# Macaron block on one core: first-pair score maxima started three block steps later, router logits of four tiles in one step

## The chip, the core and the metric

One core of a Trainium2 chip runs the whole program. The metric is device time in microseconds, and lower is better. Five engines work side by side, each through its own queue in order: PE (TensorE, matmul, with its weight loads shown as PEld), DVE (VectorE), ACT (ScalarE), POOL (GpSimd) and SP (SyncE, which here only issues DMAs). Semaphores connect them.

## The reference

The input is 8 sequences of 1024 tokens of 256 numbers, all fp32. Three layers follow each other, each on a layer norm of x:

```python
x = x + 0.5 * ffn(layernorm(x))
x = x + attention(layernorm(x))
x = x + 0.5 * ffn(layernorm(x))

# attention: 16 heads of 16
xd = (x @ W_down).reshape(b, t, h, s)
keys    = einsum('bthk,hik->bthi', xd, tokeys) * scale     # queries, values alike
attn    = softmax(einsum('bqhs,bkhs->bhqk', queries, keys))
out     = einsum('bhqk,bkhs->bqhs', attn, values).reshape(b, t, e) @ W_unify + b_unify

# ffn: one expert of 8 a token, at most 320 tokens an expert, the rest through one shared network
probs = softmax(xf @ router_w + router_b); eid = argmax(probs)
rank  = cumsum(onehot)[.., eid] - 1;       valid = rank < 320
out   = where(valid, expert[eid](xf), relu(xf @ ow1 + ob1) @ ow2 + ob2)
```

The softmax is computed with its maximum taken off, and a token's place in its expert depends on all tokens before it.

## The kernel before

Three stages follow each other: the first feed-forward layer, attention, and the second feed-forward layer. In each, the order of the instructions on PE, ACT and DVE is the order in which Python emits them (a manual schedule), so a generator's `yield` decides which work lies next to which.

**The feed-forward layers** run in blocks of 512 tokens (`Layer.blocks`, L433). A block is sixteen steps between yields: eight steps that multiply into the hidden layer (`ph_o`, L456) and eight that multiply out of it (`pe_o`, L499), where the four tiles of 128 tokens take two steps each, of 10 and of 6 matmul records. The finished rows are scattered to DRAM by a POOL DMA (L512).

**Attention** goes over 32 pairs, 8 sequences times 4 groups of 4 heads. A pair is sixteen steps `u` (called steps of attention here), and each step does two things for different pairs (`passes`, L956): the exponentials of pair n (three matmuls `psc` a head, the last of which brings in the row minima `m`, then an exponential on ACT), and the maxima of pair n + 1 (two matmuls `pm` a head, then a reduction `halves` on DVE, L1003). In between, the previous step's exponentials are multiplied with the values (`av`, L1018). After eight steps `lowest` (L931) makes the minima of half a pair, and `spread` (L944) sends them through DRAM into the rows `m` with two DMAs on SP (L948, L949). `fetch(n)` (L919) loads keys and queries of pair n with three DMAs on SP: two for keys (L926) and one for queries (L929).

**Work beside attention.** Everything else that attention needs is kept as generators in the list `beside`: `prepare` (the projections of the next sequence), `unify` (the output projection), `stats`, `biased`, and `route` (the second layer's router). Each is labelled with what its next piece needs most: ARRAY, DVE or POOL, and has a pair by which it is due. A step of attention may take one ARRAY piece (in 8 or 6 of the 16 steps of a pair, `SLOTS_OF`, L776), one DVE piece (in 6 or 8 of them), and a POOL piece if it took no ARRAY piece. What is not done when its pair ends is emitted there at once (`done_by`, L1148). A step that takes an ARRAY piece, or is one of the first two of its half pair, multiplies with the values in one go; others do it in two halves around the second group of scores.

`route(b)` (L1080) normalizes, transposes four tiles (`ptrn`, L832), multiplies them with the router's weights (`found`, L1087: 16 matmul records of 8 columns in `pl`, L1091), and again for the next four tiles. Then `places` (L270) finds the slots with two small groups of matmuls, `inside` and `behind` (L304, L326); after each, DVE waits for three additions on POOL. At last eight tiles are normalized and sent by POOL.

**The first pair.** The maxima of pair 0 have no exponentials to run beside. They are taken in 32 pieces of 4 matmuls while the last four blocks of the first feed-forward layer run, one after each block step (`first_pair`, L1183). The block steps are numbered 0 to 64; in each, one ARRAY, two DVE and one POOL piece may be taken. `prepare(0)` ends and `fetch(0)` is issued a few block steps ahead of the first piece; the yields behind `fetch(0)` set how many:

```python
                yield from prepare(0)
                fetch(0)
                yield POOL
                yield POOL
                for u in range(UNITS):
                    for order in ORDERS:
                        yield ARRAY
                        passes(None, 0, u, order, {})
```

When the blocks are done, every engine goes through a branch (L668) that skips a rarely needed rest, and `run` (L1230) starts with `fetch(1)`.

Of the kernel before, what the change touches and what calls it, by code (L numbers as in the profile page):

```python
# [40 lines left out]
def macaron(  # L41
# [80 lines left out]
    def clearing(pool, on=nc.gpsimd):  # L122

        zero = pool.tile([P, W], F32, tag="zero", name="zero")
        on.memset(zero, 0.0)
        nc.gpsimd.iota(
            zero[:, D : D + 1].bitcast(I32), pattern=[[1, 1]], base=N, channel_multiplier=1
        )
        return zero
# [10 lines left out]
    ARRAY, DVE, POOL = 0, 1, 2  # L140

    def norm_steps(name, b, mean, rstd):


        st = small.tile([P, TB, 6], F32, tag="st", name=f"st_{name}")
        mv = small.tile([P, TB, 2], F32, tag="mv", name=f"mv_{name}")
        for t in range(TB):
            nc.vector.bn_stats(st[:, t, :], xs[b][:, t, :])
            nc.vector.bn_aggr(mv[:, t, :], st[:, t, :])
            yield DVE  # L150
        nc.vector.tensor_copy(mean, mv[:, :, 0])
        v = small.tile([P, TB], F32, tag="v", name=f"v_{name}")
        nc.vector.tensor_scalar(v, mv[:, :, 1], EPS, None, ALU.add)

        half = small.tile([P, TB], I32, tag="half", name=f"half_{name}")
        nc.vector.tensor_single_scalar(
            half, v.bitcast(I32), 1, ALU.logical_shift_right
        )
        yi = small.tile([P, TB], I32, tag="yi", name=f"yi_{name}")
        nc.vector.tensor_scalar(  # L160
            yi, half, -1.0, float(0x5F3759DF), ALU.mult, ALU.add
        )
        y = yi.bitcast(F32)
        for i in range(4):
            if i % 2 == 0:
                yield DVE
            a = small.tile([P, TB], F32, tag="a", name=f"a_{name}_{i}")
            nc.vector.tensor_tensor(a, y, y, ALU.mult)
            nc.vector.scalar_tensor_tensor(a, a, -0.5, v, ALU.mult, ALU.mult)
            to = rstd if i == 3 else small.tile(  # L170
                [P, TB], F32, tag="yn", name=f"yn_{name}_{i}"
            )
            nc.vector.scalar_tensor_tensor(to, a, 1.5, y, ALU.add, ALU.mult)
            y = to
        yield POOL
# [5 lines left out]
    def normed(pool, tag, name, t, mean, rstd, on=None, numbered=False):  # L181
        xn = pool.tile([P, W if numbered else D], F32, tag=tag, name=name)
        on = on or nc.vector
        on.tensor_scalar(xn[:, :D], xt(t), mean, rstd, ALU.subtract, ALU.mult)
        if numbered:
            nc.gpsimd.tensor_copy(
                xn[:, D:].bitcast(I32), number[:, t : t + 1].to_broadcast([P, W - D])
            )
        return xn
# [571 lines left out]
    def attention(use, weights, router):  # L761
# [29 lines left out]
        def bank_v(name):  # L791

            return use.pm.tile([P, 512], F32, tag="pm", name=name)
# [17 lines left out]
        def rows_transposed(name, b, mean, rstd, used):  # L811

            def rows(q):
                return [
                    normed(
                        use.pool, "xn", f"{name}_{b}_{t}", b * TB + t, mean[:, t : t + 1],
                        rstd[:, t : t + 1], nc.gpsimd,
                    )  # L820
                    for t in range(4 * q, 4 * q + 4)
                ]

            ready = rows(0)
            yield POOL
            yield ARRAY
            for q in range(2):
                to = use.pool.tile([P, KC, 512], F32, tag="xnt", name=f"T{name}_{b}_{q}")
                for k in range(KC):
                    ps = bank(f"pt{name}_{b}_{q}_{k}")  # L830
                    for i, r in enumerate(ready):
                        nc.tensor.transpose(  # L832
                            ps[:, i * P : (i + 1) * P], r[:, k * P : (k + 1) * P], ident
                        )
                    nc.scalar.copy(to[:, k, :], ps)
                if q == 0:
                    ready = rows(1)
                yield
                yield from used(q, to)
# [240 lines left out]
        def route(b):  # L1080

            sl = slice(b * TB, (b + 1) * TB)
            mean, rstd = router.mean[:, sl], router.rstd[:, sl]
            yield from norm_steps(f"f1_{b}", b, mean, rstd)
            logits = use.pool.tile([P, TB, E], F32, tag="logits", name=f"logits1_{b}")

            def found(q, xnt):  # L1087
                pl = bank_v(f"pl_{b}_{q}")
                for i in range(4):
                    for k in range(KC):  # L1090
                        nc.tensor.matmul(  # L1091
                            pl[:, i * E : (i + 1) * E],
                            lhsT=xnt[:, k, i * P : (i + 1) * P],
                            rhs=rw_sb[:, k, :],
                            start=(k == 0),
                            stop=(k == KC - 1),
                        )
                    if i == 1:
                        yield
                nc.vector.tensor_tensor(  # L1100
                    logits[:, 4 * q : 4 * q + 4, :],
                    pl[:, : 4 * E].rearrange("p (t e) -> p t e", e=E),
                    rb_sb.unsqueeze(1).to_broadcast([P, 4, E]),
                    ALU.add,
                )
                yield ARRAY if q == 0 else DVE

            yield from rows_transposed("rn", b, mean, rstd, found)
            yield from router.places(b, logits, use.pool, bank_v, nc.gpsimd)
            for t in range(b * TB, (b + 1) * TB):  # L1110

                xn = normed(
                    use.pool, "send", f"send1_{t}", t, *router.of(t),
                    nc.gpsimd if b < B - 2 else nc.vector, numbered=True,
                )
                router.send(t, xn)
                yield POOL

        def stats(b):

            sl = slice(b * TB, (b + 1) * TB)
            yield from norm_steps(f"a{b}", b, amean[:, sl], arstd[:, sl])
# [4 lines left out]
        def afterwards(n=0):  # L1127

            for _ in range(len(later) - n):
                later.pop(0)()  # L1130
# [42 lines left out]
        def ones(i):  # L1173
            vp = use.pool.tile([P, TB * HEADS * V + S], F32, tag=f"vp{i}", name=f"vp{i}")
            nc.gpsimd.memset(vp, 1.0)
            vps.append(vp)

        def zero_rows(i):
            m = use.pool.tile([P, 512], F32R, tag=f"m{i}", name=f"m{i}")
            nc.gpsimd.memset(m.bitcast(F32), 0.0)  # L1180
            ms.append(m)

        def first_pair(others):  # L1183

            for i in range(2):
                zero_rows(i)
            ones(0)  # L1190
            zero = clearing(use.pool)

            def steps():

                for _ in range(6):
                    yield POOL
                yield DVE
                yield from stats(0)
                yield POOL
                yield from prepare(0)  # L1200
                fetch(0)
                yield POOL
                yield POOL
                for u in range(UNITS):
                    for order in ORDERS:
                        yield ARRAY
                        passes(None, 0, u, order, {})
                    if u % TB == TB - 1:
                        lowest(0, u // TB)
                    elif u % TB == 0:  # L1210
                        afterwards()
                yield DVE
                afterwards()

            beside.append([0, POOL, steps()])
            for i, _ in enumerate(others):

                if i in (10, 29, 36):

                    reload((10, 29, 36).index(i) + 1)  # L1220
                if i in (17, 36, 43):
                    again = (17, 36, 43).index(i) + 1
                    beside.append([again + 1, DVE, stats(again)])
                if i in (44, 52):
                    clear(zero, 1, *((0, SLOTS) if i == 44 else (SLOTS + SURE, ROWS)))
                for kind in (ARRAY, DVE, DVE, POOL):
                    step(kind)
            done_by(B)
# [185 lines left out]
```

## Time and profile before

| what | value |
|---|---|
| time, median of 3 runs | 2935.99 us (2933.0 to 2938.25) |
| the profiled execution's own time | 2939.6 us |
| its span, first to last instruction | 2937.9 us |
| mean granted TensorE clock | 0.981 |
| PE busy | 2799.3 us (95%) |
| DVE busy | 1883.1 us (64%) |
| ACT busy | 1375.2 us (47%) |
| POOL busy | 851.8 us (29%) |
| attention proper, first psc to last av | 660.5 to about 2450 us |

The span is 1.7 us shorter than the profiled execution's time, and that execution is 3.6 us longer than the median. The clock column of a profile is the share of full TensorE speed that was granted in a stretch; the hardware records when it changes.

### The profile page before, as it was taken

How to read it: one execution, taken by the hardware profiler on the slowest of the kernel's cores; microseconds unless marked ns; L12 is line 12 of the kernel's file. 1: busy time of each engine (PE TensorE's matmuls, PEld its weight loads, DVE VectorE, ACT ScalarE, POOL GpSimd, SP SyncE). 2: the span in 40 equal slices, each digit the busy share in tenths (PEclk: the TensorE clock that was granted, in tenths of full speed). 3: DMA queues.
4: the chain of work that ended last, by engine and by line, in shares of the span. 5: the costliest groups of instructions: out<-in, count | busy, mean ns of one | idle time of the engine just before them, and what ended most of it. 6: DMA issues, size and time to landing. Idle time of an engine off the chain costs nothing.

```text
span 2937.9 us, 56693 instructions
## 1 busy us (share of the span) xinstructions
PE 2799.3 (95%) x22066; PEld 1546.2 (53%) x22066; DVE 1883.1 (64%) x4189; ACT 1375.2 (47%) x2512; POOL 851.8 (29%) x1136
## 2 busy tenths in 40 slices
PE   4799999899999999999999999999999999999998
PEld 4567776454444444444444444444444445666775
DVE  7344223467897888888788788788788963212221
ACT  1111111207766666766766765766766663111111
POOL 3434433414001033123222321420420214432331
PEclk7799999999999999999999999999999999999999
DMA  7522553413112101301301301311321102321440
GB/s 224 152 83 78 176 187 99 161 47 121 53 58 97 67 24 60 124 24 56 128 24 52 133 24 42 125 41 39 125 80 38 39 3 73 128 61 49 150 147 28
DMA packets 163737, 251.47 MB, mean 86 GB/s; under 512 B 36737, under 2 KB 109698, under 8 KB 163458
## 3 DMA queue, kind: packets, MB, share of 16 engines
q1 hardware_dynamic: 144178, 196.93, 20.6%
q0 software_dynamic: 18432, 50.62, 5.1%
q8 instruction: 177, 2.90, 0.4%
q14 instruction: 102, 0.84, 0.1%
q10 hardware_dynamic: 848, 0.18, 0.0%
HBM read 144.10 MB, written 103.57 MB: 84 GB/s over the span
## 4 chain that ended last, share of the span: by engine, by line
PE 63%; DVE 13%; issue 1%; DMA 0%; POOL 0%; ACT 0%; POOLq 0%; DVEq 0%
PE psc L987 20%; PE av L1018 15%; DVE halves L1003 9%; PE pm L987 6%; PE pe_o L499 5%; PE ph_o L456 5%; PE pe_e L499 2%; PE ph_e L456 2%; PE pu L1063 2%; PE pxd L862 2%; PE pv L894 1%; DVE turned L1033 1%; PE pq L880 1%; PE pl L1091 1%; PE ptrn L832 0%
## 5 line engine op out<-in xcount | busy, mean ns | idle before, releaser
L1003 DVE TENSOR_REDUCE halves<-pm 128x1 f32<-128x512 f32 x2048 | 1309.3, 681 | 260.9 <-PE pm L987 239.6
L996 ACT ACTIVATE ex<-psc 128x512 f32<-128x512 f32 x2048 | 1111.4, 596 | 574.5 <-PE psc L987 570.9
L987 PE MATMUL pm<-k,q 32*128 32x512 f32 x4096 | 870.5, 448 | 50.6 <-DVE halves L1003 38.6
L987 PE MATMUL psc<-q,k 32*128 32x512 f32 x4096 | 791.8, 455 | 3.1 <-PEq L668 3.1
L1018 PE MATMUL av<-ex,vp 128*32 128x256 f32 (+1 forms) x6472 | 610.9, 449 | 0.0
L987 PEld LDWEIGHTS psc<-q,k 32*128 32x128 f32 x4096 | 326.6, 183 | 479.0 <-issue 423.1
L987 PEld LDWEIGHTS pm<-k,q 32*128 32x128 f32 x4096 | 374.9, 183 | 133.4 <-DVE halves L1003 107.3
L987 PE MATMUL psc<-m,ones_r 32*128 32x512 f32 x2048 | 406.9, 390 | 0.0
L456 PE MATMUL ph_o<-bT_o,oa 128*128 128x512 f32 x704 | 318.6, 601 | 7.1 <-DVE h_o L474 5.3
L499 PE MATMUL pe_o<-ob,h_o 128*128 128x256 f32 x1408 | 322.6, 386 | 0.0
L1041 POOL TENSOR_TENSOR ot<-turned,rec 128x256 f32<-128x256 f32 x64 | 39.7, 620 | 883.9 <-DVE rec L1036 875.6
L499 PEld LDWEIGHTS pe_o<-ob,h_o 128*128 128x128 f32 x1408 | 268.1, 193 | 48.5 <-issue 13.8
L1018 PEld LDWEIGHTS av<-ex,vp 128*32 128x32 f32 x6472 | 127.6, 108 | 298.3 <-issue 275.6
L456 PEld LDWEIGHTS ph_o<-bT_o,oa 128*128 128x128 f32 x704 | 131.2, 191 | 159.7 <-issue 147.4
L470 ACT ACTIVATE h_o<-ph_o,ob 128x512 f32<-128x512 f32 x88 | 60.5, 687 | 328.9 <-PE ph_o L456 305.0
L987 PEld LDWEIGHTS psc<-m,ones_r 32*128 32x128 f32 x2048 | 196.6, 184 | 13.0
L474 DVE TENSOR_SCALAR h_o<-ph_o,ob 128x512 f32<-128x512 f32 x88 | 65.9, 748 | 196.2 <-ACT h_o L470 179.4
L509 DVE SCALAR_TENSOR_TENSOR y_o<-pe_o,old_o 128x256 f32<-128x256 f32 x88 | 37.2, 423 | 205.8 <-PE pe_o L499 141.2
L499 PE MATMUL pe_e<-wb,h_e 128*128 128x256 f32 (+1 forms) x640 | 143.9, 381 | 0.0
L456 PE MATMUL ph_e<-bT_e,wa 128*128 128x320 f32 x512 | 140.6, 433 | 1.8 <-ACT bT_e L204 1.8
L204 ACT COPY bT_o<-pt_bT_o 128x1024 f32<-128x1024 f32 x22 | 22.3, 1012 | 250.8 <-PE pt_bT_o L200 225.9
L499 PEld LDWEIGHTS pe_e<-wb,h_e 128*128 128x128 f32 (+1 forms) x640 | 112.9, 179 | 16.4 <-issue 3.1
(183 smaller groups left out, 2385.1 us busy)
## 6 DMA issues: line engine op xcount, KB each, us to landing
k<-krows SPq DMA_DIRECT2D x64, 512.0 KB
wa<-in_w_dram SPq DMA_DIRECT2D x16, 1024.0 KB
wb<-in_w_dram SPq DMA_DIRECT2D x16, 1024.0 KB
krows<-kh SPq DMA_DIRECT2D x32, 512.0 KB
krows<-kl SPq DMA_DIRECT2D x32, 512.0 KB
q<-qrows SPq DMA_DIRECT2D x32, 512.0 KB
rows_o<-buf SPq DMA_DIRECT2D x88, 130.0 KB
x<-in_x_dram SPq DMA_DIRECT2D x8, 1024.0 KB
```

Source lines behind the costliest of these rows:

```text
L456: nc.tensor.matmul(ps[:, i * 512 : i * 512 + width], lhsT=wa[:, k, (m + i) * P : (m + i + 1) * P], rhs=xnt[:, k, c0:c1], start=(k == 0), s ...
L470: nc.scalar.activation(t[:, 0, : hi - lo], ps[:, lo - c0 : hi - c0], AF.Relu, bias=bias[:, m : m + 1],)
L474: nc.vector.tensor_scalar(t[:, 1, : hi - lo], ps[:, 512 + lo - c0 : 512 + hi - c0], bias[:, m + 1 : m + 2], 0.0, ALU.add, ALU.max,)
L499: nc.tensor.matmul(ps[lo - i * P : hi - i * P, :D], lhsT=of[:, lo - a : hi - a], rhs=w[:, m, :], start=(m == 0), stop=(m == MC - 1),)
L509: nc.vector.scalar_tensor_tensor(y[:n, :], ps[:n, :D], 0.5, olds[i][:n, :], ALU.mult, ALU.add)
L862: nc.tensor.matmul(ps, lhsT=wd_sb[:, k, m * P : (m + 1) * P], rhs=xnt[:, k, :], start=(k == 0), stop=(k == KC - 1),)
L987: nc.tensor.matmul(ps, lhsT=lhs, rhs=rhs, start=(len(left) + 1 == todo[kind, h, "of"]), stop=not left,)
L996: nc.scalar.activation(ex, ps, AF.Exp, scale=S ** -0.5)
L1003: nc.vector.tensor_reduce(halves[m][:, t, half, h : h + 1], ps, AX.X, ALU.max, negate=True)
L1018: nc.tensor.matmul(avs[n, q][32 * h : 32 * h + 32, cols], lhsT=vps[b % 2][:, at : at + 2 * S], rhs=ex[:, cols], start=(c == 0), stop=(c == ...
L1041: nc.gpsimd.tensor_tensor(outs_t[q][:, :, at : at + S].rearrange("p (t a) s -> p a t s", t=4), by[:, :, :S].rearrange("p (a t) s -> p a t ...
L1063: nc.tensor.matmul(ps[:, i * D : (i + 1) * D], lhsT=outs[b, g, q][:, at : at + P], rhs=wu_sb[:, g, :], start=(g == 0), stop=(g == G // 2 - 1),
```

## The change

Two edits. In `first_pair`, five POOL yields instead of two follow `fetch(0)`, so that the first of the 32 pieces of maxima comes three block steps later, and so do all pieces after it. In `route`, `found` no longer yields in the middle of its four tiles, so that its 16 matmul records are one ARRAY piece, where they were two of 8 records; a router pass takes two ARRAY pieces fewer, and whatever stands behind it in `beside` moves up.

```diff
--- before.py
+++ after.py
@@ -1095,8 +1095,6 @@
                             start=(k == 0),
                             stop=(k == KC - 1),
                         )
-                    if i == 1:
-                        yield
                 nc.vector.tensor_tensor(
                     logits[:, 4 * q : 4 * q + 4, :],
                     pl[:, : 4 * E].rearrange("p (t e) -> p t e", e=E),
@@ -1199,8 +1197,9 @@
                 yield POOL
                 yield from prepare(0)
                 fetch(0)
-                yield POOL
-                yield POOL
+
+                for _ in range(5):
+                    yield POOL
                 for u in range(UNITS):
                     for order in ORDERS:
                         yield ARRAY
```

## The prediction

> **What bounds the kernel now.** I read the page's chain first, then PE's and SP's timelines around the end of the first layer, then the clock by windows.
>
> ```profile
> PE 63%; DVE 13%; issue 1%; DMA 0%; POOL 0%; ACT 0%; POOLq 0%; DVEq 0%
> ```
>
> The set end is PE's, with DVE second, so I price both edits on PE and ask where DVE ends a wait. PE at the first pair (timeline: start, length, instruction, idle before it and its releaser):
>
> ```profile
> 541.02 5.78 PE L499 MATMUL pe_o<-ob,h_o 128*128 128x256 f32 x26
> 554.43 1.22 PE L987 MATMUL pm<-k,q 32*128 32x512 f32 x4 [7.63 <-DMA q<-qrows]
> 555.58 2.93 PE L499 MATMUL pe_o<-ob,h_o 128*128 128x256 f32 x6
> ...
> 645.93 0.92 PE L987 MATMUL pm<-k,q 32*128 32x512 f32 x4
> 646.78 10.63 PE L499 MATMUL pe_o<-ob,h_o 128*128 128x256 f32 x48
> 660.51 0.79 PE L987 MATMUL psc<-q,k 32*128 32x512 f32 x2 [3.10 <-PEq L668]
> ```
>
> PE stands 7.63 us for the queries, and the blocks behind the first piece stand with it. The last piece comes 48 block records ahead of the end; then come the branch's 3.1 us. SP meanwhile:
>
> ```profile
> 648.76 0.33 SPq L948 DMA_DIRECT2D mrows<-lowturned  x1
> 650.17 0.64 SPq L949 DMA_DIRECT2D m<-mrows  x1
> 652.89 0.81 SPq L926 DMA_DIRECT2D k<-krows  x2
> 653.75 0.42 SPq L929 DMA_DIRECT2D q<-qrows  x1
> ```
>
> Keys and queries of pair 1 are asked for only behind the last minima. Their packets in the trace end at 659.1 us, one straggler at 660.5; PE wants them at 660.6. Two waits end within 0.2 us of each other, and one is not seen.
>
> Windows of the granted clock (length, busy time and count of PE, PEld, DVE, ACT, POOL, then PEclk):
>
> ```profile
> 553.71:557.12 3.41, 2.69 (x8) 1.80 (x9) 1.29 (x2) 0.00 (x0) 0.00 (x0) 0.50 0.00 1
> 557.13:560.53 3.40, 3.40 (x10) 1.90 (x9) 1.26 (x3) 0.00 (x0) 1.00 (x1) 0.50 0.00 0
> 560.54:563.94 3.40, 3.40 (x9) 2.36 (x7) 0.44 (x1) 0.00 (x0) 0.00 (x0) 0.50 0.39 83
> ...
> 1506.03:1509.44 3.41, 3.31 (x36) 2.17 (x36) 2.88 (x7) 1.37 (x3) 0.62 (x1) 1.00 0.87 332
> 1509.44:1512.85 3.41, 3.41 (x20) 1.08 (x12) 1.56 (x3) 1.17 (x3) 0.00 (x0) 0.50 0.06 10
> ...
> 1048.09:1051.88 3.79, 3.79 (x41) 2.15 (x38) 3.69 (x11) 2.63 (x6) 0.45 (x1) 1.00 0.92 313
> 1051.88:1056.09 4.21, 4.11 (x37) 2.15 (x36) 3.10 (x7) 2.13 (x5) 0.17 (x1) 1.00 0.26 99
> 1507.93:1513.70 5.77, 5.67 (x39) 2.63 (x38) 3.31 (x7) 2.29 (x5) 0.19 (x1) 0.70 0.21 75
> ```
>
> The clock changes only on a grid of 3.413 us. After the long stall PE ran at half speed for 9.5 us more. And at 1509.4 it fell to half although PE was busy 3.31 of the 3.41 us before. The last two rows are the same step of attention (second of a pair, with 8 router records) at full speed and hit: 5.77 against 4.21 us.
>
> **First edit: the maxima three block steps later.** Nothing is added. Pieces and their DMAs keep their order on DVE and SP; `fetch(0)` and the earlier work stay. Three block steps (6 + 10 + 6 records at 3.46/16 = 0.216 us, 4.75 us) pass ahead of the first piece, so 7.63 becomes 2.9. Two more row scatters fall into the busy DMA time before the queries land (128 KB each at the 390 GB/s there, 0.3 us each): +0.4. The half-speed time shrinks: the next window then starts in a block of 10 records instead of short maxima, so I expect full speed one window earlier; half of 3.4 us, say -2 (0 to -3). The last piece has three further steps ahead of it (10 + 6 + 10 records, +5.6) for the 22 taken away, so it starts at 645.93 + 0.86 + 0.4 - 2 = 645.2. The SP chain hangs on that piece: pair 1's queries land at 659.1 + 0.86 + 0.4 - 2 = 658.4. PE has only 22 records left (4.75 us) and is through the branch at about 654; it then waits for those queries. So the gain is 660.6 - 658.4 = 2.2, not 7. The half clock at the start of attention (until 666.3 now) stays, as PE is idle as long or longer: -0.3 at most. **-2.5 us** (-7 if the keys came earlier than I think, +1.5 if no half-speed window is saved). The later PE stall of 1.30 us on DVE (at 598.8 us, followed by a window at half clock) stays: statistics and maxima meet there in both orders. Nobody else waits behind the new PE wait: the first `psc` pair, then everything, is PE's.
>
> **Second edit: order of the pieces.** I counted by hand, from `queue`, `SLOTS_OF` and `due`, which piece falls into which step, and took each step's length from the timeline (first `psc` of one to first `psc` of the next). Lengths repeat to 0.05 us: plain 2.94; with 8 router records 3.78, and 4.21 where DVE lags at a half pair's start; with transposes 3.82; with `pxd`, `pq`, `pu` 4.71, `pv` 4.78; two whole-`av` steps at a half pair's start 2.47 + 3.6.
> - First half of a router pair (pair 27): 3.77 + 4.23 + 3.82 for router, router, transposes becomes 4.70 + 3.82 + 4.71. Eight more records cost 0.93 (their pace in the timeline); DVE catches up meanwhile: +1.4.
> - Second half: two router steps go, `inside` moves to the start, where DVE is already late (minima, transposition, reciprocal), `behind` comes in from the next pair. `behind` at such a place took 2.47 + 4.34 + 3.86 + 3.12 in pair 28 against 2.47 + 3.60 + 3.99 + 3.03 in pair 29 without it: +0.7 from that row.
> - Next pair: `behind` is gone and, POOL's sends going first, the next `prepare` starts one ARRAY piece later: -2.4 (-0.9 in pair 28, which has no `prepare`).
> - Pair after it: its last `pv` no longer fits and is emitted at the pair's end: +2.2; then DVE catches up and the two short steps behind it lose some of their lag: -1.0 (no row shows it; 0 to -1.5).
>
> Sum +0.9 for five passes, +1.1 for the sixth; the last, in pair 31, I put at +0.5: **+6 us** (-3 to +13). POOL's later normalization has about 1 us of cover before its transposes; without it they stall that long.
>
> **Second edit: the clock.** What does the grid react to? I gave every PE record its share of the array: a `pe_o` record counts 0.216 us whole; an `av` record of 256 columns and a score record a quarter of that (32 of 128 columns, 32 of 128 rows), a router record of 8 columns nothing. Summed by grid window from 480 to 2450 us, the five windows after which the clock fell hold 0, 26, 35, 35 and 36% of a full window; the lowest after which it stayed holds 39%. Two of the five lie in attention, one around a router piece.
>
> The Trainium skill (TensorE: Matmul & The Clock Gate, "Why this matters for your kernels") says that PE gaps over about 3 us bring the half clock; 16 router records in a row leave no gap (the hit window above was idle 0.1 us), so by it the piece costs nothing more and the sum ends at +3.5. By the row, a piece of 1.9 us without array work, amid work at about 65% of the array, falls under 37% as soon as a window holds 1.44 us of it: (3.41 - 1.92 + 2 x 0.48)/3.41 = 0.72. Sliding the grid over the real records with 0.93 us put in gives 0.68 for twelve pieces and 0.54 for pair 31's two: 9.2 hits; the single one of before goes. A hit costs 5.77 - 4.21 = 1.55 (1.44 at the other). 8.2 x 1.5 = **+12.3 us** (0 if the page is right, +20 if all are hit). I follow the row: it is this kernel's own.
>
> **Sum.** -2.5 + 6 + 12.3 = +15.8. The profiled execution took 2939.6 (span 2937.9 and 1.7 around it): 2955.4. It was 3.6 above the median of 2936.0, so 2951.8, rounded 2952.
>
> **Rivals.**
> 1. The clock does not mind: only -2.5 + 6, 2939.5. For it: 27 of 28 router pieces pass today. Against: those are half as long.
> 2. Faster: the query stall goes and nothing takes its place: 4.75 and 2 us of clock reach the end. It needs pair 1's queries to land before PE is through the branch (about 654), so decides at an SP issue before 648, where SP's row shows 652.9; with pieces rearranged at the good end (-3): 2936 - 6.75 - 3 = 2926.
> 3. The shift doesn't do what it says: pieces left over when the blocks end, run bare. Counting puts the last piece into block step 61 of 64, so I give it little; 3 pieces of 1.3 us of DVE would make 2956 with the rest.
>
> **How the numbers follow.** My forecast has 0.65, rivals 0.17, 0.14 and 0.04. 0.2% (5.9 us), about what a measurement of this kernel can tell, puts "same" between 2930 and 2942. Faster: most of rival 2, 0.13. Same: most of rival 1, the forecast's low end, 0.19. Slower: 0.68. The range reaches from rival 1's lower part to all pieces hit: 2933 to 2964; the forecast's own is 2942 to 2963.
>
> **What would show it.** Right: stall before the first `pm` near 3 us; a new wait of some 4 us on `q<-qrows` at the first `pm` of attention; PEclk at 0.50 in windows after most router pieces, and the mean clock at 0.976 or so (28 us more at half of 2938); router pairs (7, 11, ...) about 2 us longer apart from hits. Wrong: PEclk 1.00 throughout attention, or attention starting near 654.

## The result and the profile after

| | before | after |
|---|---|---|
| median, 4 runs each on one chip | 2937.12 us (2933.0 to 2939.59) | 3019.88 us (3016.62 to 3028.83) |
| ratio, 95% interval | | 1.0288 [1.0263, 1.0313] |
| span of the profiled execution | 2937.9 us | 3017.8 us |
| mean granted clock | 0.981 | 0.966 |

The change costs 83 us, five times the forecast's 15.8 and outside its range. The page's chain of the kernel after has a new member, POOL:

```profile
PE 61%; DVE 11%; POOL 3%; issue 2%; DMA 1%; ACT 0%; POOLq 0%; SPq 0%; DVEq 0%; ACTq 0%
```

3% of 3017.8 us is about 90 us. GpSimd stood at 0% before.

**The first pair** went much as worked out. PE's timeline after (start, length, instruction, idle before it and its releaser), and below it SP's:

```profile
540.05 10.53 PE L499 MATMUL pe_o<-ob,h_o 128*128 128x256 f32 x48
553.36 0.73 PE L987 MATMUL pm<-k,q 32*128 32x512 f32 x4 [2.79 <-DMA q<-qrows]
...
642.22 5.01 PE L499 MATMUL pe_o<-ob,h_o 128*128 128x256 f32 x22
648.30 0.50 PE L987 MATMUL psc<-q,k 32*128 32x512 f32 x2 [1.06 <-DVEq L668]
656.79 0.79 PE L987 MATMUL pm<-k,q 32*128 32x512 f32 x2 [8.00 <-DMA q<-qrows]
```

```profile
644.39 0.33 SPq L948 DMA_DIRECT2D mrows<-lowturned  x1
647.01 0.64 SPq L949 DMA_DIRECT2D m<-mrows  x1
650.58 0.80 SPq L926 DMA_DIRECT2D k<-krows  x2
651.44 0.42 SPq L929 DMA_DIRECT2D q<-qrows  x1
```

The 7.63 us stall has shrunk to 2.79, attention starts 12.2 us earlier (648.30 against 660.51), and 8.00 us of that go at once into a wait for pair 1's queries, because SP still asks for them behind the last minima. After that wait the clock is at half until 663.4, and pair 1 starts 3.4 us earlier than before. That last number is no firm gain: against the same trace of before, kernels with the old start (the router edit alone, the product on VectorE in before, the long piece alone, all below) have pair 1 at -3.2, -3.1 and +2.3 us, and kernels with the new one anywhere from -3.4 to +4.5.

**From pair 7 on it is lost.** I took the time from one pair's first `psc` to the next pair's, in both traces. Differences (after less before, us) of the pairs in which the router works, of the pair behind it, and of the two behind that:

| sequence's router in pair | 7 | 11 | 15 | 19 | 23 | 27 |
|---|---|---|---|---|---|---|
| the router's pair | +3.9 | +4.0 | +5.1 | +1.3 | +1.3 | +4.2 |
| the next pair | **+7.2** | **+7.9** | **+7.8** | **+7.9** | **+7.1** | **+14.4** |
| the one after | +1.7 | +1.7 | +1.5 | +2.1 | +2.1 | -0.2 |
| the fourth | -0.2 | -0.2 | -0.2 | -0.2 | -0.2 | 0.0 |

With the -3.4 of the start and +3.6 behind pair 31's start this is the whole 79.9 us of the two spans. The second row alone holds 52.2, where the forecast had -2.4 a pair. It sits in the third step of attention of the pair (12.04 us in pair 8, before 3.28) and in the one behind it: 9.8 us in the two in pair 8, 66.9 in all six pairs, of which later steps give some back. The list of waits (what waits for what: us in total, times, longest), first before, then after:

```profile
PE pm L987 <- DVE halves L1003: 38.6, 75, 1.3
DVE ho L1053 <- POOL ot L1041: 1.5, 2, 0.7
```

```profile
PE pm L987 <- DVE halves L1003: 95.7, 92, 12.9
DVE ho L1053 <- POOL ot L1041: 53.3, 8, 12.7
```

PE waits 57 us more for the maxima on DVE; DVE waits 52 us more for POOL's product `ot`, the last step of the division by the softmax's sums. A transpose `ho` on VectorE is behind that product, and the maxima behind the transpose. The timelines of POOL, DVE and PE in pair 8, after:

```profile
1099.10 1.12 POOL L361 DMA_INDIRECT buf<-send,slot  x1 [0.56 <-DVE lost L345]
...
1106.38 1.09 POOL L361 DMA_INDIRECT buf<-send,slot  x1 [0.28 <-POOL send L186]
1109.84 1.22 POOL L184 TENSOR_SCALAR send<-x,mean,rstd 128x256 f32<-128x256 f32 x1 [2.36 <-DMA buf<-send,slot]
...
1119.80 1.09 POOL L361 DMA_INDIRECT buf<-send,slot  x1 [0.28 <-POOL send L186]
1120.90 0.20 POOL L186 COPY send<-number 128x4 int32<-128x4 int32 x1
1121.05 0.62 POOL L1041 TENSOR_TENSOR ot<-turned,rec 128x256 f32<-128x256 f32 x1
```

```profile
1106.72 0.25 DVE L1036 RECIPROCAL rec<-turned 128x16 f32<-128x16 f32 x1
...
1121.71 0.71 DVE L1053 STREAM_TRANSPOSE ho<-ot 128x512 f32<-128x512 f32 x1 [7.74 <-POOL ot L1041]
```

```profile
1114.65 0.50 PE L987 MATMUL pm<-k,q 32*128 32x512 f32 x1
1123.05 0.79 PE L987 MATMUL pm<-k,q 32*128 32x512 f32 x1 [7.90 <-DVE halves L1003]
```

`ot` could have run at 1107.0, when its reciprocal `rec` was there. It ran at 1121.05, behind all eight sends of the router's rows, four of which were issued after it was ready. Each is a normalization of 1.22 us, a copy of 0.18 and a DMA issue of 1.09, and back to back they repeat every 2.77 us. Before, the same two engines there read:

```profile
1106.52 0.62 POOL L1041 TENSOR_TENSOR ot<-turned,rec 128x256 f32<-128x256 f32 x1 [5.26 <-DVE rec L1036]
```

```profile
1113.32 0.70 DVE L1053 STREAM_TRANSPOSE ho<-ot 128x512 f32<-128x512 f32 x1
```

POOL was not yet sending when `ot` became ready, and `ho` found it done 6 us earlier. In the code, `ordered` (L52) holds PE, ACT and DVE; POOL is not in it, so POOL's order is not the order of emission. The planner that builds the program sets it. The matmuls `behind`, which the sends need, moved from the tenth step of pair 8 to the thirteenth of pair 7, and the planner laid all eight sends ahead of an `ot` that is emitted before five of them. In the order of emission only three would stand ahead of it, and the third was issued by 1104.7, before `ot` was ready.

**The clock** took what was left. The granted clock by windows in pair 8 (length, busy time and count of PE, PEld, DVE, ACT, POOL, then PEclk, DMA share, GB/s), after:

```profile
1113.98:1117.39 3.41, 1.17 (x13) 0.35 (x11) 0.00 (x0) 1.09 (x2) 2.81 (x4) 1.00 0.34 116
1117.39:1120.80 3.41, 0.00 (x0) 0.00 (x0) 0.00 (x0) 0.00 (x0) 3.08 (x4) 0.50 0.12 41
1120.80:1124.22 3.42, 1.17 (x10) 0.52 (x10) 2.20 (x4) 0.00 (x0) 0.86 (x3) 0.50 0.11 39
1124.22:1127.63 3.41, 3.41 (x25) 1.22 (x26) 2.63 (x6) 1.76 (x4) 0.00 (x0) 0.50 0.00 0
```

The stall behind the sends brings 10.2 us at half clock (17.1 in pair 28). Most of that passes while PE stands; the work in the step behind pays 1.1 to 1.9 us for it. Apart from these, six of the fourteen router pieces are followed by a fall of the clock, one of them in pair 7:

```profile
1062.78:1066.20 3.42, 3.42 (x37) 2.39 (x30) 2.65 (x5) 1.70 (x4) 0.00 (x0) 1.00 0.00 0
1066.20:1069.61 3.41, 3.41 (x27) 1.77 (x28) 1.48 (x3) 1.09 (x2) 0.00 (x0) 0.50 0.00 0
```

PE was busy for the whole of the window ahead of the fall. The router's 16 records, from 1064.3, are what it did in its last 1.9 us.

### The profile page after: what moved, and what is told of

Same layout as the page of the kernel before. It is cut to its first block, busy times and chain, and to the rows that moved or that the text cites. A ratio compares the mean times of both kernels' runs of the same rounds, so it can differ in the third digit from the quotient of the medians.

```text
span 3017.8 us, 56779 instructions
## 1 busy us (share of the span) xinstructions
PE 2823.2 (94%) x22106; PEld 1553.4 (51%) x22106; DVE 1887.6 (63%) x4189; ACT 1375.5 (46%) x2512; POOL 851.7 (28%) x1136
## 4 chain that ended last, share of the span: by engine, by line
PE 61%; DVE 11%; POOL 3%; issue 2%; DMA 1%; ACT 0%; POOLq 0%; SPq 0%; DVEq 0%; ACTq 0%
PE psc L987 19%; PE av L1018 15%; DVE halves L1003 8%; PE pm L987 6%; PE pe_o L499 5%; PE ph_o L456 5%; PE pe_e L499 2%; PE ph_e L456 2%; PE pxd L862 2%; POOL buf L361 1%; POOL send L184 1%; PE pu L1063 1%; PE pv L894 1%; PE pq L880 1%; PE pl L1091 1%
## 5 line engine op out<-in xcount | busy, mean ns | idle before, releaser
L987 PE MATMUL psc<-q,k 32*128 32x512 f32 x4096 | 803.4, 461 | 1.2 <-DVEq L668 1.1
L1018 PE MATMUL av<-ex,vp 128*32 128x256 f32 (+1 forms) x6512 | 624.2, 455 | 0.0
```

Of the source, the lines that this page charges most:

```text
L987: nc.tensor.matmul(ps, lhsT=lhs, rhs=rhs, start=(len(left) + 1 == todo[kind, h, "of"]), stop=not left,)
L1018: nc.tensor.matmul(avs[n, q][32 * h : 32 * h + 32, cols], lhsT=vps[b % 2][:, at : at + 2 * S], rhs=ex[:, cols], start=(c == 0), stop=(c == ...
```

## The experiments

They ran in three groups, each on a chip of its own, beside its own runs of the kernel before (medians 2945.55, 2942.12 and 2937.38 us). Single runs of one kernel spread over some 10 to 20 us there, so I compare by the ratios and their intervals; microseconds behind a ratio are that ratio times the median of before in its group.

The theories at the start: (A) most of the loss is POOL's queue, a smaller part the clock after long router pieces; (B) it is the clock, and the waits follow from it; (C) the two edits disturb each other.

### Each edit alone

The delay alone (x1_delay_only):

```diff
                 fetch(0)
-                yield POOL
-                yield POOL
+                for _ in range(5):
+                    yield POOL
```

> The first edit alone (five POOL yields behind fetch(0), router pieces of 8 records as before). Theory of the SP chain: the stall on the queries shrinks to about 3 us, attention's first psc starts about 12 us earlier, and its first pm waits some 8 us for the queries of pair 1; 3.4 us faster than before (what pair 1's start shows in the changed kernel), about 2933.5 us. Rival, the two edits act on each other: anything outside 2930 to 2937. POOL's row and the clock say nothing here.

Measured: 2940.81 us, 0.9984 [0.9968, 1.0000], -4.7 us; the interval reaches zero. Its trace has the stall at 2.90 us and the wait for the queries at 8.19, as expected, but attention starts 9.7 us earlier, not 12, and pair 1 only 0.5.

The router's 16 records in one step, without the delay (x2_router_only):

```diff
-                    if i == 1:
-                        yield
```

> The second edit alone (16 router records in one piece, two POOL yields behind fetch(0)). If the edits add: the changed kernel and 3.4 us, about 3023 us, with waits of DVE ho on POOL ot of 8 to 13 us in pairs 8, 12, 16, 20, 24, 28. If they act on each other, the time is outside 3017 to 3030.

Measured: 3023.33 us, 1.0267 [1.0240, 1.0295], +78.6 us, with the wait of `ho` for `ot` at 54.1 us. The loss is the second edit's; the first brings a few microseconds at most. (C) falls as a main cause: -0.0016 and +0.0267 make +0.0251, against +0.0288 [0.0263, 0.0313] for both. With these intervals an effect of one edit on the other of some 10 us is not excluded.

### The long piece without the new order

The kernel before with the 16 records in one piece and a step that takes an ARRAY slot and does nothing ahead of it, so that everything behind keeps its place (x3_blank_ahead):

```diff
             def found(q, xnt):
+                yield
                 pl = bank_v(f"pl_{b}_{q}")
...
-                    if i == 1:
-                        yield
```

> The second edit with one empty ARRAY piece ahead of each group of 16 records, so that 16 records are one piece but all that follows keeps its step (first edit left out). Theory POOL's row (places ready earlier, so that eight sends of 2.8 us stand ahead of the product ot that DVE's ho and then PE wait for): no such wait is left; only hits of the clock by the 16-record pieces, about 7 of 14 at 1.5 us, plus less DVE lag: +6 to +14 us, about 2946. Rival clock (the long pieces themselves cost most of the 83 us, through half speed): +40 or more, about 2980.

Measured: 2963.81 us, 1.0066 [1.0044, 1.0088], +19.4 us. The wait for `ot` is at 1.5 us, as before. Six of 14 pieces are followed by half speed; one of them by windows:

```profile
2205.43:2208.85 3.42, 3.42 (x38) 2.81 (x36) 1.80 (x4) 1.50 (x3) 0.00 (x0) 1.00 0.08 16
2208.85:2212.26 3.41, 3.41 (x29) 1.20 (x28) 1.74 (x3) 1.08 (x2) 0.00 (x0) 0.50 0.00 0
```

So the long pieces cost about a quarter of the loss, more than expected, and (B) falls as the main cause. Against the router edit alone, only the places of the pieces differ, and that is 1.0267 - 1.0066 = 0.0201, 59 us.

### The change with POOL's old order

The kernel after, with a blank ARRAY step inside `places`, ahead of the part that ends in the sends, so that these come when the second `ot` is through (x4_behind_back):

```diff
-            yield from router.places(b, logits, use.pool, bank_v, nc.gpsimd)
+            arrays = 0
+            for kind in router.places(b, logits, use.pool, bank_v, nc.gpsimd):
+                arrays += kind == ARRAY
+                if kind == ARRAY and arrays == 2:
+                    yield ARRAY
+                yield kind
```

> Both edits, with one empty ARRAY piece ahead of the second group of matmuls of places (behind), so that behind and the sends come in the pair after, where they were before; POOL's queue of router sends and products is then that of the kernel before. Theory POOL's row: the waits of ho on ot go and with them 50 to 60 us; what stays is the first edit's -3.4, the clock's hits (about +10) and the changed places (about 0 to +8): 2940 to 2955 us. Rival clock or rival placement (the earlier inside and router pieces are what costs): above 2990 us.

Measured: 2959.37 us, 1.0045 [1.0029, 1.0060], +13.3 us. POOL's timeline in pair 8, and the list of waits:

```profile
1116.61 0.62 POOL L1041 TENSOR_TENSOR ot<-turned,rec 128x256 f32<-128x256 f32 x1 [14.49 <-DVE rec L1036]
1147.64 0.62 POOL L1041 TENSOR_TENSOR ot<-turned,rec 128x256 f32<-128x256 f32 x1 [30.41 <-DVE rec L1036]
...
1156.53 1.12 POOL L361 DMA_INDIRECT buf<-send,slot  x1 [0.56 <-DVE lost L345]
```

```profile
PE pm L987 <- DVE halves L1003: 43.8, 87, 1.6
DVE ho L1053 <- POOL ot L1041: 1.5, 2, 0.7
```

Both waits are back near before's, and 1.0288 - 1.0045 = 0.0243 of the loss went with them, 71 us. What is left, +13.3, is about the sum of the delay (-4.7) and the long pieces (+19.4). This is the run that carries theory A: every instruction of the change is in it, and only the part of `places` that ends in the sends is back in the tenth step of pair 8, where the kernel before has it, with what stands behind it moved to match. So it moves `behind` along with POOL's order; the next run tells the two apart.

### The product on VectorE

A second way to free `ot` from the sends is to give it to another engine:

```diff
-            nc.gpsimd.tensor_tensor(
+            nc.vector.tensor_tensor(
                 outs_t[q]
```

In the kernel after (x6_ot_dve):

> The changed kernel, with the product ot of the division on VectorE (0.7 us there, twice a pair) in place of GpSimd: nothing of attention stands behind the router's sends any more. Theory (the wait behind the sends, about 60 us in six pairs, is the larger cause; the clock after pieces of 16 records, about 18 us, the other; the first edit gives 4): the wait of VectorE's transpose ho for ot is gone from the list of waits, pair 8 is no longer than before by more than 1 us, and the time is 1.003 to 1.009 of before (2954 to 2972 us). Rival (the order of the other pieces in the pair after the router's costs, GpSimd's wait is only seen beside it): pairs 8, 12 ... 28 stay 5 us or more longer, time above 1.02.

Measured: 2985.57 us, 1.0154 [1.0131, 1.0176]. The wait is gone and pair 8 is 2.1 us shorter than before, with all pieces where the change has them: it is not the place of `behind` that costs. But the time is well above what was expected, so I needed the control, the same edit in the kernel before (x7_before_ot_dve):

> The kernel before with the product ot of the division on VectorE, the control for x6_ot_dve and x12_wide_ot. Theory (what those two still lose is the price of ot on VectorE, which paces attention there, 0.8 us a pair in the 31 pairs that follow pair 0): 20 to 30 us over before, 1.007 to 1.010, each plain pair longer by 0.5 to 1.1 us. Rival (what they lose is a third cost of the change): under 1.003.

Measured: 2985.85 us, 1.0144 [1.0112, 1.0176], +42 us, more than the 20 to 30 expected. Most plain pairs grow by 0.5 to 1.1 us, as expected; pairs 7 and 11 grow by 13.8 and 7.8, with half-speed windows behind router pieces, and elsewhere, that the kernel before does not have. The pair of runs says that with `ot` on DVE the change costs next to nothing (1.0154 against 1.0144), but it says it with a clock that is disturbed in both. As a sum it is weaker evidence than the blank step, and it is a poor remedy: DVE paces attention as well.

### Is it the array's share, or the number of short instructions?

The kernel of "the long piece without the new order", with the router's matmuls 64 columns wide in place of 8. The weights get zeros behind them (`rw_flat`); 56 columns of each result are not used (x11_wide):

```diff
-                            pl[:, i * E : (i + 1) * E],
+                            pl[:, i * 64 : (i + 1) * 64],
                             lhsT=xnt[:, k, i * P : (i + 1) * P],
-                            rhs=rw_sb[:, k, :],
+                            rhs=rw_flat[:, k * E : k * E + 64],
```

> The kernel before with the router's 16 records in one step and a blank step ahead (as in x3_blank_ahead), but with each of the router's matmuls in attention 64 columns wide in place of 8: 56 of them are not used, the number of instructions and of weight loads stays. Theory (the clock falls where the array's columns fill too little of a 3.4 us window; 16 records of 64 columns bring the window back over the limit): none of the 14 pieces is followed by a half-speed window, the mean clock is again near 0.981 in place of 0.974, and the time is 0.998 to 1.002 of before. Rival (the clock falls on the count of short instructions or weight loads in a row): 5 to 8 of the pieces are hit as with 8 columns, 1.005 to 1.010. Third: wider matmuls last longer and are paid in the step itself, 1.002 to 1.005 with no hit.

Measured: 2946.35 us, 1.0017 [1.0001, 1.0032]. The mean clock was expected near 0.981 and is 0.994 in the profiled run, but 0.978 to 0.994 over all twelve, much as before's own runs (0.977 to 0.994), so it tells nothing. A piece takes 2.00 us in place of 1.95, with the same 16 matmuls and 16 weight loads, and none of the 14 is followed by half speed. The granted clock around the same piece of pair 27 (here it begins at 2194.1):

```profile
2192.00:2195.41 3.41, 3.41 (x37) 1.95 (x30) 2.69 (x6) 2.17 (x4) 0.00 (x0) 1.00 0.21 71
2195.41:2198.83 3.42, 3.42 (x43) 1.90 (x42) 2.01 (x4) 1.35 (x3) 0.00 (x0) 1.00 0.02 4
```

PE is as busy as in the run with 8 columns; what differs is how much the array has to do. So the clock's part is 1.0066 - 1.0017 = 0.0049, 14 us (6 to 22 by the two intervals). The rest, 0.0017 or 5 us, goes with the long step itself; of the 2.7 us by which pair 31 starts later in this trace, 1.2 stand there at the start already.

Both remedies at once in the kernel after, `ot` on VectorE and wide router matmuls (x12_wide_ot):

> The changed kernel with both costs taken away: the product ot on VectorE, and the router's matmuls in attention 64 columns wide (56 unused). Theory (two causes and no third): the delay's gain of 3 to 5 us is left, less what ot costs on VectorE, 0.997 to 1.002 of before. Rival (a third cost, such as the order of the pieces in the pairs around the router): 1.003 to 1.010.

Measured: 2969.25 us, 1.0102 [1.0080, 1.0125]. This is at the upper end of the rival's figure, but it carries the price of `ot` on DVE: its plain pairs are 0.5 to 1.1 us longer, as in the control, and tell nothing of a third cost. So I tried the two remedies again with POOL's work left where it was.

### Is there a third cost?

The blank step inside `places` and the wide router matmuls, in the kernel after (x14_behind_back_wide):

> The changed kernel with both causes taken away and GpSimd's work unchanged: the blank step ahead of the second part of the places (so that the sends stand behind ot again, as in x4_behind_back), and the router's matmuls in attention 64 columns wide. Theory (two causes and no third): no half-speed window after a piece of 16, the delay's gain of 3 to 5 us left, 0.998 to 1.001 of before. Rival (a third cost in the order of the pieces, up to the +6 us of the prediction): 1.002 to 1.005.

Measured: 2947.65 us, 1.0032 [1.0019, 1.0045], +9.4 us. This is on the side of the rival. The theory had left out what the long step itself costs (0.0017 in x11_wide); beyond that 4 us are left, or 9 if the delay's gain is real, each good to some 6 us. So a third cost is likely, and small. No router piece is followed by half speed. By pairs, only two are longer than before by over 2 us (pair 0, which pays for its early start, aside): pair 7 by 2.7 and pair 11 by 4.4, both in the fourth and fifth step. DVE's, POOL's and PE's timelines in pair 7 (the lines stand three further down in this kernel):

```profile
1060.24 0.38 DVE L171 TENSOR_TENSOR a_a<-yi_a 128x8 f32<-128x8 f32 x1
1060.65 0.17 DVE L172 SCALAR_TENSOR_TENSOR a_a<-a_a,v_a 128x8 f32<-128x8 f32 x1
...
1061.26 0.73 DVE L172 SCALAR_TENSOR_TENSOR a_a<-a_a,v_a 128x8 f32<-128x8 f32 x1
1062.03 0.65 DVE L176 SCALAR_TENSOR_TENSOR yn_a<-a_a,yn_a 128x8 f32<-128x8 f32 x1
```

```profile
1061.24 2.78 POOL L918 TENSOR_TENSOR x<-x,bu 128x256 f32<-128x256 f32 x4
```

```profile
1063.33 0.73 PE L990 MATMUL pm<-k,q 32*128 32x512 f32 x1 [1.64 <-DVE halves L1006]
```

Newton's steps of the next normalization (the iterations for its inverse square root) meet POOL's additions of the bias to x. Two of them take 0.73 and 0.65 us in place of 0.17, each until the addition beside it ends; PE waits 1.64 us for the maxima, and the clock falls in the window behind. In the kernel before the same steps stand in the same place, the fourth step of pair 7, and take 0.17 us each: POOL's additions come at 1071.37 there, behind them. So it is POOL's work that moved. The kernel after shows the same wait, 1.62 us in pair 7, and the steps there are 1.2 us longer in pairs 7 and 11. That this is the whole third cost was read from traces and not tested by itself.

### A better start

SP's queue was what ate the first edit's earlier start. The last minima need not be spread when the blocks end: pair 0's own first step can do it, behind the fetch of pair 1. The first edit alone, with this besides (x9_delay_spread_last):

```diff
                 yield DVE
-                afterwards()
 
             beside.append([0, POOL, steps()])
```

> The first edit alone (five steps between fetch and the first minima), and the last minima's spread (mrows and m) left to pair 0's own first step, so that on SP's queue the fetch of pair 1 comes ahead of them. Theory (the 8 us that pair 0's first pm waits for its q rows are SP's queue): the wait falls from 8 us to under 3, and the time is 6 to 12 us under before, 0.996 to 0.998. Rival (the wait is the transfer itself, or something else ends as late): no more than the first edit alone gives, 3 to 5 us, 0.998 to 0.9995.

Measured: 2933.81 us, 0.9968 [0.9954, 0.9983], -9.4 us against the kernel before, and faster than both kernels. SP's and PE's timelines:

```profile
609.35 0.82 SPq L926 DMA_DIRECT2D k<-krows  x2
610.22 0.42 SPq L929 DMA_DIRECT2D q<-qrows  x1
...
651.72 0.32 SPq L948 DMA_DIRECT2D mrows<-lowturned  x1
654.38 0.64 SPq L949 DMA_DIRECT2D m<-mrows  x1
```

```profile
642.03 5.02 PE L499 MATMUL pe_o<-ob,h_o 128*128 128x256 f32 x22
648.11 0.50 PE L987 MATMUL psc<-q,k 32*128 32x512 f32 x2 [1.07 <-DVEq L668]
648.24 0.50 PE L987 MATMUL pm<-k,q 32*128 32x512 f32 x2
```

The wait of 8.00 us is gone, and pair 1 starts 13.0 us earlier than before. Pair 1's queries are asked for at 610 us, not at 651: with no late minima ahead of it on SP, the fetch leaves 41 us earlier. The control is the same edit with the old two yields (x10_spread_last):

> The kernel before with the last minima's spread left to pair 0's own first step and the delay as before, the control for x9. Theory (before, the way to the first score is bound by the branch of the first pair's maxima, not by SP's queue, so the spread matters only with the delay): within 2 us of before, 0.9993 to 1.0007. Rival (x9's gain over the first edit alone is the spread's own): 0.996 to 0.998.

Measured: 2939.02 us, 0.9999 [0.9981, 1.0017]. With the spread alone the first stall stays (7.62 us in its trace), so the blocks end as late as before, and only the branch is shorter, 1.07 in place of 3.10. With the delay alone the blocks end earlier and PE waits for the queries. It takes both to start pair 1 by 13 us earlier, far outside the -3.2 to +2.3 of kernels with the old start. The ratios alone (0.9984, 0.9999, and 0.9968 for both) have intervals too wide to show that the whole is more than its parts.

In its profile the better start gives 6 of its 13 us back from pair 19 on, in half-speed windows. So the last run adds the wide router matmuls, in the two halves that the kernel before has (x13_spread_last_wide):

> x9_delay_spread_last with the router's matmuls in attention 64 columns wide, in the two halves that the kernel before has. Theory: the 6 us that x9 gave back after pair 18 were half-speed windows behind pieces of the router; none is left, and the time is 11 to 15 us under before, 0.995 to 0.9965. Rival (the wide matmuls cost in their steps what the windows gain): as x9, 0.9965 to 0.998.

Measured: 2931.25 us, 0.9975 [0.9962, 0.9987]. No router piece is hit, and pairs 1 to 27 start 14.5 to 17.6 us earlier than before, but a fall of the clock in pair 27, around the small matmuls of `places`, costs 5.4 us. By the ratio the wide matmuls add nothing to the better start: the gain expected of them is not there.

## Why the prediction was wrong

**First edit: right in its waits, its sum not settled.** Forecast -2.5; the run with this edit alone has -4.7 [-9.4, 0], and the starts of pair 1 in the traces scatter by more than that. The first stall came at 2.79 (forecast 2.9). The wait on `q<-qrows`, forecast at some 4 us, came at 8.00, for PE was through the branch at 648.3, not 654: the branch took 1.06 and not the 3.1 of before, and the last piece came at 641.55, not 645.2, because the half speed behind the stall lasted 3.4 us, not 13.7, and the window at 601.5, which I had let stay, is gone too. (The two scatters, put at +0.4, make 0.6 by their own figures.) None of this could be kept, as the queries set the end: 656.8, forecast 658.4.

**Order of the pieces: the step that failed.** "Next pair: `behind` is gone and, POOL's sends going first, the next `prepare` starts one ARRAY piece later: -2.4". The -2.4 is there: from the tenth step of pair 8 on, the trace has -2.6. But the clause "POOL's sends going first" was priced only at the transposes of `prepare`, with "about 1 us of cover". I did not ask what else on POOL's queue stands behind eight sends of 2.77 us. It is `ot`, then `ho` on DVE, then the maxima, then PE: 9.8 to 10.6 us in two steps of each of five pairs, 15.6 in pair 28. It could have been seen in the trace of before: there `ot` runs at 1106.52, with `ho` 6 us behind it, and eight sends of 2.77 us, which were to move up to just there, are 22 us. My own counting of steps treated POOL as following the order of emission, which holds for PE, ACT and DVE alone; in that order `ot` would not have waited. The runs put this step at 59 us (router alone against long piece alone) and 71 us (change against change with the old order); the trace's 66.9 lies between.

The other three terms were of the right size or small: the half pairs of the router +2.1 forecast, +1.3 in pairs 19 and 23 and some 4 in pairs 7, 11, 15 and 27, where the clock and the Newton steps are in it; the pair after +2.2 less 1.0 forecast, +1.7 less 0.2 measured.

**The clock: right in mechanism, and in size as far as is known.** Forecast +12.3 from 9.2 hits of 1.5 us; measured +14 (8 columns against 64, long piece alone), with six hits of 14 that last one to three windows each, so fewer and longer. Two more pairs of runs differ in these columns alone: with `ot` on VectorE 1.0154 - 1.0102 = 0.0052, 15 us (6 to 25), but with the sends back 1.0045 - 1.0032 = 0.0013, 4 us (-2 to 10). The limit of 36 to 39% is one trace's: counted in the same way, the trace of the long piece alone has falls behind windows of up to some 39% and none behind some of 34%. The rule on gaps in the Trainium skill (TensorE: Matmul & The Clock Gate, "Why this matters for your kernels") would have put it at 0; the trace has a fall behind windows without a gap. Rival 1, which was that rule, is wrong. What I left out is that each new stall brings its own 10 us of half clock, so that a wait of 7.9 us costs 9.8 in two steps.

**The rivals and the signs.** Rival 2 was right in what it needs, an SP issue before 648: the better start has it at 610 and gains 9.4 us, where 6.75 was worked out. Rival 3 did not happen. Of the signs named, the stall near 3 us and the longer router pairs appeared; the new wait was twice as long as said, six pieces in fourteen is not "most", and the mean clock fell to 0.966, not 0.976, since the stalls lower it as well. None of the signs would have shown POOL's part. The list of waits does, in its line for `ho`.

**The sum**, by the experiments: delay -5, long piece as such +5, clock +14, POOL's queue +59 to +71, together +73 to +85; both edits measured 83 in the result's runs. The two ends of POOL's queue are good to some 10 us each, so the sum leaves room for the third cost and does not measure it. That cost stays open: the Newton steps are its only sign (pairs 7 and 11, together 7 us longer in one profile), and no run took them away.

## What to carry to other kernels

When a step moves, list what stands behind it on every queue that is not in the order of emission, and follow each to the engine that sets the end: eight sends that nothing waited for, on an engine that is 29% busy, cost more than everything else here. Before moving work earlier at a boundary, find every wait that ends there; where two end within a microsecond, take away both (0.9984 and 0.9999 alone, 0.9968 together). A matmul with few columns is not free even where PE has no gap: pieces of 16 with 8 columns were followed by half clock in six to eight of 14 places, with 64 columns in none.

## What the runs showed of the hardware

- The clock falls behind windows of 3.41 us in which PE was busy throughout, if much of that is weight loads with 8 columns each. Of 14 such pieces of 16 records, six were hit in each of three kernels (the change, the router edit alone, the long piece alone), seven in the change with POOL's old order and eight in the change with `ot` on DVE. With 64 columns none of 14, 14, 14 and 28 pieces was hit in the four kernels that have them, at 2.00 us a piece of 16 against 1.95 (the 28 are pieces of 8).
- In stalls with PE idle for 7.7 to 8.2 us, half clock began at a window's edge within the stall and lasted 10.2 us, in five places; in the sixth PE was idle for 12.9 us, and it lasted 17.1.
- Small DVE instructions on 128x8 elements took 0.64 to 0.73 us in place of 0.17 while POOL's additions on 128x256 elements ran, four times in the attention of the kernel after and four in x14_behind_back_wide, and not once in that of the kernel before.
- In the first group the 21 runs of the kernel before lay between 2938.88 and 2955.31 us, with mean clocks from 0.976 to 0.994: the time and the clock of one kernel differ from run to run. With nine to twelve runs of a kernel the intervals were 0.25 to 0.36% wide.
